# Linear attention in pairs of chunks, values held twice, and steps of attention and projection alternating

## The chip, the core and the metric

The kernel runs on one core of one Trainium2 chip. The metric is the device time of one execution in microseconds (us). The kernel before takes 1238.45 us, the median of three runs (1237.87 to 1241.02).

## What is computed

One transformer layer over x of 1 x 2048 x 512. The first part is causal linear attention on the normalized x: 16 query heads, four key/value heads (each shared by four query heads), head size 128. Queries and keys are rotated by their position (rotary map) and then go through elu + 1; a state of 128 x 128 and a vector z grow with every token:

```
q = rotary(Wq xn); k = rotary(Wk xn); v = Wv xn        # xn = layernorm(x)
qf = elu(q) + 1;   kf = elu(k) + 1
for each token s:
    state = state + outer(kf[s], v[s]);  z = z + kf[s]
    o[s] = (qf[s] . state) / (qf[s] . z + 1e-6)
x = x + Wo o
```

The second part is a mixture of 32 experts and 32 zero experts on the normalized result: softmax scores plus a bias, the top 8 per token, at most 256 tokens per expert, silu(g) * u between two matrix products, and a weighted sum added to x.

## The kernel before

*Tiling.* The 2048 tokens are cut into four blocks of 512 (`NSB`, `SB`), a block into four chunks of 128 (`NC`, `P`), and a chunk into two halves of 64 (`T`). Inside a block there is a loop over `G` = 4 groups; a group is one key/value head with its `R` = 4 query heads. Everything in the attention is f32, and a matrix product of f32 runs on TensorE as two passes, which the trace records separately.

*A block.* `norm_block` normalizes x and transposes it (xT). `values` (L266) makes the values of a chunk for all four groups (pv) and ScalarE copies them to SBUF (`va`, L274). `project` (L299) does a group: the keys pk (L305, four matmuls of 128 x 512), then `rope_feature` (L277) on them, a running sum over the tokens (zT, L309), then four times the queries of a head, pq (L317, four matmuls each), each with `rope_feature`. Then the denominators: VectorE multiplies queries by zT (qz, L325) and TensorE sums over the head with a matrix of ones (pd, L328). VectorE adds 1e-6 and takes the reciprocal (rd, L331 and L332). These are written to DRAM (`recip`, L333) and read back four times, once per chunk, spread over all 128 partitions (`rds`, L337, 256 KB each); `rds` has three buffers. Write and reloads go through SP's DMA queue, which works in order.

*`rope_feature`* takes a projection in PSUM to a feature in SBUF. VectorE multiplies by the cosine (L282), multiplies each half of 64 rows by the sine and puts it into the other half's place (L283, L284), adds (L285) and takes the minimum with 0 (L286); ScalarE takes exp of that (L287); VectorE forms max(., 0) + exp (L288).

*Attention of a chunk.* `by_token` transposes the keys of a group (L294), and ScalarE copies them (kk, L296). `attend` (L343) does a chunk: scores of each half against itself (L355, two matmuls, each on 64 columns of the array); the increments of the state, once for the first half (64 rows) and once for the whole chunk (128 rows) (L361), both in the same PSUM tile as the scores; the state's additions on VectorE (L366); the causal mask on the scores (at, L370); the output po per half, first from the state (L376, full array), then from the values (L379, 64 rows of the array); and VectorE's product with the reciprocals (oT, L381).

*After the groups.* `output` (L383) multiplies by Wo (px, L391, 16 matmuls), adds x (L393) and normalizes again; `route` (L404) transposes (prt, L408), makes the router's logits (pl, L413), softmax and top 8 (sel, L431) and each token's place in its expert's list (pp, L446 and L447); `list_further` writes the lists with indirect DMAs. These are interleaved with the fourth group of a block. After the last block come the experts (L561 on), which this change doesn't touch.

*Buffers.* pk, pq, px and pv share two PSUM buffers (`p_pj`); scores with state increments have two (`p_sc`), po one per half (`p_o`), transposes one (`p_tr`), and pd, pl and pp together one (`p_ms`).

*Order.* Each engine takes its instructions in the order that the built program gives. A framework decides it: it keeps data dependences and buffer turns, and apart from these a scheduler with its own estimates arranges the instructions of an engine, starting from the order of the source. In the source (main loop, L501 on) the projection of the next group, g + 1, comes in one piece ahead of the four chunks of group g; with g = 3 it is the next block's norm and first group.

Of the kernel before, what the change touches and what calls it, by code (L numbers as in the profile page):

```python
# [9 lines left out]
F32 = mybir.dt.float32  # L10
# [3 lines left out]
ALU = mybir.AluOpType  # L14
# [4 lines left out]
P = 128  # L19
# [33 lines left out]
def linattn_moe(  # L53
# [122 lines left out]
    with ExitStack() as ph:  # L176
        wts = ph.enter_context(tc.tile_pool(name="wts", bufs=1))
        blk = ph.enter_context(tc.tile_pool(name="blk", bufs=2))
# [3 lines left out]
        rdp = ph.enter_context(tc.tile_pool(name="rdp", bufs=NC - 1))  # L182
        rowp = ph.enter_context(tc.tile_pool(name="rowp", bufs=NC))
        vap = ph.enter_context(tc.tile_pool(name="vap", bufs=NC))
# [6 lines left out]
        p_sc = ph.enter_context(tc.tile_pool(name="p_sc", bufs=2, space=PSUM))  # L191
# [8 lines left out]
        def load_block(sb):  # L200
            xs = [load_row(sb * NC + c, "n") for c in range(NC)]
            if sb == 0:
                first_weights()
            cs = blk.tile([P, SB], F32, tag="cs", name=f"cs_{sb}")
            nc.sync.dma_start(out=cs, in_=cosT[:, ts(sb, SB)])
            sn = blk.tile([P, SB], F32, tag="sn", name=f"sn_{sb}")
            nc.sync.dma_start(out=sn, in_=sinT[:, ts(sb, SB)])
            return xs, cs, sn
# [56 lines left out]

        def values(sb, c, xT):  # L266
# [6 lines left out]
            va = vap.tile([P, G, HD], F32, tag="va", name=f"va_{sb}_{c}")  # L273
            nc.scalar.copy(va, pv)  # L274
            return va

        def rope_feature(dst, ps, sb, name):  # L277
# [3 lines left out]
            hh = HD // 2  # L281
            nc.vector.tensor_tensor(dst, ps, cs, ALU.mult)  # L282
            nc.vector.tensor_tensor(b[:hh], ps[hh:], sn[hh:], ALU.mult)  # L283
            nc.vector.tensor_tensor(b[hh:], ps[:hh], sn[:hh], ALU.mult)  # L284
            nc.vector.tensor_tensor(dst, dst, b, ALU.add)  # L285
            nc.vector.tensor_scalar(b, dst, 0.0, None, ALU.min)  # L286
            nc.scalar.activation(b, b, AF.Exp)  # L287
# [11 lines left out]
        def project(sb, g, xT):  # L299
# [11 lines left out]
            if sb < NSB - 1:  # L311
                nc.scalar.copy(zend[:, g : g + 1], zT[:, SB - 1 :])
            qT = qkp.tile([P, R, SB], F32, tag="qT", name=f"qT_{sb}_{g}")
            for r in range(R):
# [4 lines left out]
                rope_feature(qT[:, r, :], pq, sb, f"q{sb}_{g}_{r}")  # L319

# [18 lines left out]
            return kT, qT, rds  # L339
# [3 lines left out]
        def attend(sb, g, c, proj, kk, va, oT):  # L343
# [3 lines left out]
            n = f"{sb}_{g}_{c}"  # L347
            halves = range(P // T)
            half = [slice(c * P + a * T, c * P + (a + 1) * T) for a in halves]
            old = state[g]  # L350
            psk = p_sc.tile([P, R * T + 2 * HD], F32, tag="sc", name=f"psk_{n}")
            psc = psk[:, : R * T].rearrange("p (r t) -> p r t", r=R)
            pst = psk[:, R * T :].rearrange("p (a d) -> p a d", a=2)
            for a in halves:
                nc.tensor.matmul(psc[ts(a, T)], lhsT=kT[:, half[a]], rhs=qT[:, :, half[a]],  # L355
                                 start=True, stop=True)

            n_new = 2 if sb < NSB - 1 or c < NC - 1 else 1
            for a in range(n_new):
                to = slice(0, (a + 1) * T)  # L360
                nc.tensor.matmul(pst[:, a], lhsT=kk[to, c], rhs=va[to, g, :], start=True, stop=True)  # L361
            new = stp.tile([P, 2, HD], F32, tag=f"st{g}", name=f"state_{n}")
            if old is None:
                nc.vector.tensor_copy(new, pst)
            else:
                nc.vector.tensor_tensor(new[:, :n_new], pst[:, :n_new],  # L366
                                        old[:, 1:].to_broadcast([P, n_new, HD]), ALU.add)
            state[g] = new
            at = tmp.tile([P, R, T], F32, tag="at", name=f"at_{n}")
            nc.vector.tensor_tensor(at, psc, causal.unsqueeze(1).to_broadcast([P, R, T]), ALU.mult)  # L370
            pos = []
            for a in halves:
                po = p_o.tile([P, R, T], F32, tag=f"o{a}", name=f"po_{n}_{a}")
                before_half = (old[:, 1] if old is not None else None, new[:, 0])[a]
                if before_half is not None:
                    nc.tensor.matmul(po, lhsT=before_half, rhs=qT[:, :, half[a]], start=True, stop=False)  # L376
                pos.append((po, before_half is None))
            for a, (po, first) in enumerate(pos):
                nc.tensor.matmul(po, lhsT=va[ts(a, T), g, :], rhs=at[ts(a, T)], start=first, stop=True)  # L379
            for a, (po, first) in enumerate(pos):  # L380
                nc.vector.tensor_tensor(oT[:, :, half[a]], po, rds[c][:, :, ts(a, T)], ALU.mult)  # L381
# [22 lines left out]
        def route(ch, xw):  # L404
# [19 lines left out]
            sb_ = sml.tile([P, EZ], F32, tag="sbias", name=f"sbias_{ch}")  # L424
# [3 lines left out]
            rest = sml.tile([P, EZ], F32, tag="rest", name=f"rest_{ch}")  # L428
# [22 lines left out]
            if ch >= LISTED:  # L451

                free = sml.tile([P, E], F32, tag="hi", name=f"free_{ch}")
# [15 lines left out]
            hi = sml.tile([P, E], F32, tag="hi", name=f"hi_{ch}")  # L469
            nc.vector.tensor_scalar(hi, pos, float(C2), float(P * NCOL - 1), ALU.is_ge, ALU.mult)  # L470
            mi = sml.tile([P, E], F32, tag="mi", name=f"mi_{ch}")
# [378 lines left out]
```

## Time and profile before

| what | us |
|---|---|
| runs: median (lowest to highest) | 1238.45 (1237.87 to 1241.02) |
| the profiled execution itself | 1237.05 |
| its span on the engines | 1235.3 |
| first matmul / last instruction of px (end of the attention) | 9.6 / 886.7 |
| busy, whole span: TensorE / VectorE / ScalarE / GpSimd | 1050.5 / 637.9 / 130.2 / 219.7 |
| pq (L317) / px (L391), 512 records each, busy | 230.3 / 232.4 |
| po from state (L376) / from values (L379), busy | 76.8 / 54.6 |
| scores (L355) / state increments (L361), busy | 50.5 / 56.7 |
| VectorE's oT (L381), 128 instructions, busy | 50.1 |
| ScalarE's exp of a feature (L287), one | 0.630 |

The profile is that of one execution. "Busy" is the time in which an engine has an instruction in work; matmuls overlap with their neighbours, so their own durations add up to more than the time from one start to the next. A "wait" names what was last to release an idle engine; it is inferred from the semaphores' events. PEld is TensorE's loading of weights, and DMA queues are named after the engine that issues (SPq is SyncE's). In the page's row of slices the span is cut in 40 parts, and each digit is a busy share in tenths.

### The profile page before, as it was taken

How to read it: one execution, taken by the hardware profiler on the slowest of the kernel's cores; microseconds unless marked ns; L12 is line 12 of the kernel's file. 1: busy time of each engine (PE TensorE's matmuls, PEld its weight loads, DVE VectorE, ACT ScalarE, POOL GpSimd, SP SyncE). 2: the span in 40 equal slices, each digit the busy share in tenths (PEclk: the TensorE clock that was granted, in tenths of full speed). 3: DMA queues.
4: the chain of work that ended last, by engine and by line, in shares of the span. 5: the costliest groups of instructions: out<-in, count | busy, mean ns of one | idle time of the engine just before them, and what ended most of it. 6: DMA issues, size and time to landing. Idle time of an engine off the chain costs nothing. (4 is left out here: it accounts for less than half of the span.)

```text
span 1235.3 us, 13580 instructions
## 1 busy us (share of the span) xinstructions
PE 1050.5 (85%) x4410; PEld 530.9 (43%) x4410; DVE 637.9 (52%) x1553; ACT 130.2 (11%) x256; POOL 219.7 (18%) x254
## 2 busy tenths in 40 slices
PE   5999999999999899999999999999737765672772
PEld 2444444444444444444444444444312554441440
DVE  4888874358888435888843388834322111110110
ACT  1111110011121001112100111100011100110000
POOL 4000001430000343000034200023353121211211
PEclk9999999999999999999999999999967877786887
DMA  9411212100121210012321112340572484967224
GB/s 346 151 16 33 69 49 55 52 26 13 34 77 40 60 52 27 13 35 58 75 61 52 61 45 67 102 59 27 167 254 74 109 273 149 319 187 235 45 39 156
DMA packets 90840, 116.26 MB, mean 94 GB/s; under 512 B 12493, under 2 KB 47309, under 8 KB 90672
## 3 DMA queue, kind: packets, MB, share of 16 engines
q1 hardware_dynamic: 74640, 93.53, 25.5%
q0 software_dynamic: 10336, 12.51, 5.2%
q10 hardware_dynamic: 5760, 8.92, 2.0%
q8 instruction: 55, 0.90, 0.3%
q14 instruction: 49, 0.40, 0.1%
HBM read 101.35 MB, written 20.96 MB: 99 GB/s over the span
## 5 line engine op out<-in xcount | busy, mean ns | idle before, releaser
L317 PE MATMUL pq<-xT,wq 128*128 128x512 f32 x512 | 230.3, 599 | 10.1 <-DVE rb_q L284 10.1
L391 PE MATMUL px<-wo,oT 128*128 128x512 f32 x512 | 232.4, 599 | 0.0
L166 POOL DMA_INDIRECT slots<-tok,ai x120 | 117.6, 980 | 501.5 <-DVE ai L485 468.9
L317 PEld LDWEIGHTS pq<-xT,wq 128*128 128x128 f32 x512 | 94.4, 190 | 138.5 <-issue 107.3
L391 PEld LDWEIGHTS px<-wo,oT 128*128 128x128 f32 x512 | 93.9, 191 | 98.1 <-issue 97.6
L728 PE MATMUL pu<-xeT,gu 128*128 128x224 f32 (+1 forms) x352 | 69.4, 367 | 11.0 <-DVE xeT L656 9.7
L376 PE MATMUL po<-qT,state 128*128 128x256 f32 x248 | 76.8, 402 | 2.2 <-DVE oT L381 1.9
L728 PEld LDWEIGHTS pu<-xeT,gu 128*128 128x128 f32 x352 | 65.4, 230 | 15.4 <-issue 13.1
L393 DVE TENSOR_TENSOR x<-px,x 128x512 f32<-128x512 f32 x16 | 11.1, 692 | 113.6 <-PE px L391 98.8
L381 DVE TENSOR_TENSOR oT<-po,rds 128x256 f32<-128x256 f32 x128 | 50.1, 414 | 33.7 <-PE po L379 18.8
L305 PE MATMUL pk<-xT,wk 128*128 128x512 f32 x128 | 63.5, 627 | 0.7 <-ACT xT L263 0.7
L242 POOL TENSOR_TENSOR lnr<-lnv,mhalf 128x1 f32<-128x1 f32 (+1 forms) x20 | 13.3, 664 | 255.0 <-DVE lnv L240 228.8
L271 PE MATMUL pv<-wv,xT 128*128 128x512 f32 x128 | 57.7, 598 | 0.0
L361 PE MATMUL psk<-va,kk 64*128 64x128 f32 (+1 forms) x248 | 56.7, 323 | 0.0
L287 ACT ACTIVATE rb_q<-rb_q 128x512 f32<-128x512 f32 x64 | 40.3, 630 | 155.4 <-DVE rb_q L286 155.1
L376 PEld LDWEIGHTS po<-qT,state 128*128 128x128 f32 x248 | 41.2, 189 | 35.6 <-issue 21.7
L379 PE MATMUL po<-at,va 64*128 64x256 f32 x256 | 54.6, 428 | 0.0
L355 PE MATMUL psk<-qT,kT 128*64 128x256 f32 x256 | 50.5, 404 | 0.0
L361 PEld LDWEIGHTS psk<-va,kk 64*128 64x128 f32 (+1 forms) x248 | 36.8, 186 | 31.6 <-issue 23.8
L643 POOL DMA_INDIRECT acc<-y,idx x17 | 25.9, 1524 | 130.0 <-ACTq L778 40.0
L672 PE MATMUL pu_b<-gu,xeT_b 128*32 128x256 f32 x512 | 40.2, 424 | 10.0 <-issue 9.5
L325 DVE TENSOR_TENSOR qz<-qT,zT 128x512 f32<-128x512 f32 x64 | 42.4, 687 | 11.1 <-PE pd L328 10.6
(180 smaller groups left out, 1135.1 us busy)
## 6 DMA issues: line engine op xcount, KB each, us to landing
gu<-in_wgu_dram SPq DMA_DIRECT2D x32, 1024.0 KB
rds<-recip SPq DMA_DIRECT2D x64, 256.0 KB
dn<-in_wdn_dram SPq DMA_DIRECT2D x32, 512.0 KB
rows<-xw ACTq DMA_DIRECT2D x16, 272.0 KB
xn<-in_x_dram SPq DMA_DIRECT2D x16, 256.0 KB
wq<-in_wqT_dram SPq DMA_DIRECT2D x4, 1024.0 KB
wo<-in_woT_dram SPq DMA_DIRECT2D x4, 1024.0 KB
x<-in_x_dram SPq DMA_DIRECT2D x16, 256.0 KB
```

The lines of the kernel that those rows point to most:

```text
L166: nc.gpsimd.indirect_dma_start(out=slots[k][:, :], out_offset=bass.IndirectOffsetOnAxis(ap=ai[:, k : k + 1], axis=0), in_=tok[:, ch : ch + 1],
L271: nc.tensor.matmul(pvf, lhsT=xT[:, k, ts(c, P)], rhs=wv[:, k, :], start=(k == 0), stop=(k == KD - 1))
L305: nc.tensor.matmul(pk, lhsT=wk[:, k, ts(g, HD)], rhs=xT[:, k, :], start=(k == 0), stop=(k == KD - 1))
L317: nc.tensor.matmul(pq, lhsT=wq[g][:, k, ts(r, HD)], rhs=xT[:, k, :], start=(k == 0), stop=(k == KD - 1))
L325: nc.vector.tensor_tensor(qz, qT[:, :, cc], zT[:, cc].unsqueeze(1).to_broadcast([P, R, P]), ALU.mult)
L355: nc.tensor.matmul(psc[ts(a, T)], lhsT=kT[:, half[a]], rhs=qT[:, :, half[a]], start=True, stop=True)
L361: nc.tensor.matmul(pst[:, a], lhsT=kk[to, c], rhs=va[to, g, :], start=True, stop=True)
L376: nc.tensor.matmul(po, lhsT=before_half, rhs=qT[:, :, half[a]], start=True, stop=False)
L379: nc.tensor.matmul(po, lhsT=va[ts(a, T), g, :], rhs=at[ts(a, T)], start=first, stop=True)
L381: nc.vector.tensor_tensor(oT[:, :, half[a]], po, rds[c][:, :, ts(a, T)], ALU.mult)
L391: nc.tensor.matmul(px, lhsT=oTs[h // R][:, h % R, ts(c, P)], rhs=wo[h // R][:, h % R, :], start=(h == 0), stop=(h == H - 1))
L728: nc.tensor.matmul(pu[:, a, :m], lhsT=weights[e][0][:, k, a, c, :], rhs=xeT[:, k, :m], start=(k == 0), stop=(k == KD - 1))
```

## The change

Line numbers here are those of the changed file.

- Attention is done on pairs of chunks (`attending`). Scores of both chunks go to one PSUM tile (`p_sc`, now one buffer; four matmuls, L365), the increments of the state to another (`p_st`), and po of both chunks to one tile per half.
- The values are held twice (`vas`, four fixed tiles): once as before, and once with the first 64 tokens of the chunk only and zeros in the other 64 rows (cleared once by GpSimd, L271). So both increments of a chunk come from one matmul of 128 x 256 on the full array (L370). ScalarE makes two copies (L280, L281).
- In `rope_feature` ScalarE copies the two halves crossed (L288, L289), VectorE multiplies 128 rows by the sine in one instruction (L291), and relu(-x) on ScalarE (L293) takes the place of VectorE's minimum; exp then has scale -1 (L294). The sine is loaded in two halves, exchanged (L208, L209).
- `project` and `attend` become generators, `projecting` and `attending`, whose steps the loop takes in turn: the first pair's scores and states, k of the next group, the first pair's outputs, q0, q1, the second pair's scores and states, q2, q3, the second pair's outputs, and last the denominators with the reciprocal, its DMA write and the reloads (L339 to L346). Where g = 3, the outputs and the routing stand among these.
- Buffers: cosine and sine (`blk`) one instead of two, `rds` two instead of three, and one for several small tiles of the router (`sml`).

The core of the diff:

```diff
-        blk = ph.enter_context(tc.tile_pool(name="blk", bufs=2))
+        blk = ph.enter_context(tc.tile_pool(name="blk", bufs=1))
...
-        rdp = ph.enter_context(tc.tile_pool(name="rdp", bufs=NC - 1))
+        rdp = ph.enter_context(tc.tile_pool(name="rdp", bufs=2))
         rowp = ph.enter_context(tc.tile_pool(name="rowp", bufs=NC))
-        vap = ph.enter_context(tc.tile_pool(name="vap", bufs=NC))
+        vap = ph.enter_context(tc.tile_pool(name="vap", bufs=1))
...
-        p_sc = ph.enter_context(tc.tile_pool(name="p_sc", bufs=2, space=PSUM))
+        p_sc = ph.enter_context(tc.tile_pool(name="p_sc", bufs=1, space=PSUM))
+        p_st = ph.enter_context(tc.tile_pool(name="p_st", bufs=1, space=PSUM))
...
-            nc.sync.dma_start(out=sn, in_=sinT[:, ts(sb, SB)])
+            for i in range(2):
+                nc.sync.dma_start(out=sn[ts(i, HD // 2)], in_=sinT[ts(1 - i, HD // 2), ts(sb, SB)])
...
+        vas = [vap.tile([P, G, 2, HD], F32, name=f"va_{c}") for c in range(NC)]
+        for va in vas:
+            nc.gpsimd.memset(va[T:, :, 0, :], 0.0)
...
-            va = vap.tile([P, G, HD], F32, tag="va", name=f"va_{sb}_{c}")
-            nc.scalar.copy(va, pv)
-            return va
+            nc.scalar.copy(vas[c][:, :, 1, :], pv)
+            nc.scalar.copy(vas[c][:T, :, 0, :], pv[:T])
...
         def rope_feature(dst, ps, sb, name):
             _, cs, sn = blocks[sb]
             b = tmp.tile([P, SB], F32, tag="rb", name=f"rb_{name}")
             hh = HD // 2
+            nc.scalar.copy(b[:hh], ps[hh:])
+            nc.scalar.copy(b[hh:], ps[:hh])
             nc.vector.tensor_tensor(dst, ps, cs, ALU.mult)
-            nc.vector.tensor_tensor(b[:hh], ps[hh:], sn[hh:], ALU.mult)
-            nc.vector.tensor_tensor(b[hh:], ps[:hh], sn[:hh], ALU.mult)
+            nc.vector.tensor_tensor(b, b, sn, ALU.mult)
             nc.vector.tensor_tensor(dst, dst, b, ALU.add)
-            nc.vector.tensor_scalar(b, dst, 0.0, None, ALU.min)
-            nc.scalar.activation(b, b, AF.Exp)
+            nc.scalar.activation(b, dst, AF.Relu, scale=-1.0)
+            nc.scalar.activation(b, b, AF.Exp, scale=-1.0)
             nc.vector.scalar_tensor_tensor(dst, dst, 0.0, b, ALU.max, ALU.add)
...
-        def project(sb, g, xT):
+        def projecting(sb, g, xT):
...
+            yield
             qT = qkp.tile([P, R, SB], F32, tag="qT", name=f"qT_{sb}_{g}")
...
                 rope_feature(qT[:, r, :], pq, sb, f"q{sb}_{g}_{r}")
+                yield
...
-            return kT, qT, rds
+            projs[sb, g] = kT, qT, rds
+            yield
...
-        def attend(sb, g, c, proj, kk, va, oT):
+        def attending(sb, g, c0, proj, kk, oT):
             kT, qT, rds = proj
-            n = f"{sb}_{g}_{c}"
+            n = f"{sb}_{g}_{c0}"
+            chunks = range(2)
             halves = range(P // T)
-            half = [slice(c * P + a * T, c * P + (a + 1) * T) for a in halves]
-            old = state[g]
-            psk = p_sc.tile([P, R * T + 2 * HD], F32, tag="sc", name=f"psk_{n}")
-            psc = psk[:, : R * T].rearrange("p (r t) -> p r t", r=R)
-            pst = psk[:, R * T :].rearrange("p (a d) -> p a d", a=2)
-            for a in halves:
-                nc.tensor.matmul(psc[ts(a, T)], lhsT=kT[:, half[a]], rhs=qT[:, :, half[a]],
-                                 start=True, stop=True)
-            n_new = 2 if sb < NSB - 1 or c < NC - 1 else 1
-            for a in range(n_new):
-                to = slice(0, (a + 1) * T)
-                nc.tensor.matmul(pst[:, a], lhsT=kk[to, c], rhs=va[to, g, :], start=True, stop=True)
-            new = stp.tile([P, 2, HD], F32, tag=f"st{g}", name=f"state_{n}")
-            if old is None:
-                nc.vector.tensor_copy(new, pst)
-            else:
-                nc.vector.tensor_tensor(new[:, :n_new], pst[:, :n_new],
-                                        old[:, 1:].to_broadcast([P, n_new, HD]), ALU.add)
-            state[g] = new
-            at = tmp.tile([P, R, T], F32, tag="at", name=f"at_{n}")
-            nc.vector.tensor_tensor(at, psc, causal.unsqueeze(1).to_broadcast([P, R, T]), ALU.mult)
-            pos = []
-            for a in halves:
-                po = p_o.tile([P, R, T], F32, tag=f"o{a}", name=f"po_{n}_{a}")
-                before_half = (old[:, 1] if old is not None else None, new[:, 0])[a]
-                if before_half is not None:
-                    nc.tensor.matmul(po, lhsT=before_half, rhs=qT[:, :, half[a]], start=True, stop=False)
-                pos.append((po, before_half is None))
-            for a, (po, first) in enumerate(pos):
-                nc.tensor.matmul(po, lhsT=va[ts(a, T), g, :], rhs=at[ts(a, T)], start=first, stop=True)
-            for a, (po, first) in enumerate(pos):
-                nc.vector.tensor_tensor(oT[:, :, half[a]], po, rds[c][:, :, ts(a, T)], ALU.mult)
+            half = [[slice((c0 + i) * P + a * T, (c0 + i) * P + (a + 1) * T) for a in halves] for i in chunks]
+            psc = p_sc.tile([P, 2, R, T], F32, tag="sc", name=f"psc_{n}")
+            for i in chunks:
+                for a in halves:
+                    nc.tensor.matmul(psc[ts(a, T), i], lhsT=kT[:, half[i][a]], rhs=qT[:, :, half[i][a]],
+                                     start=True, stop=True)
+            pst = p_st.tile([P, 2, 2, HD], F32, tag="st", name=f"pst_{n}")
+            for i in chunks:
+                nc.tensor.matmul(pst[:, i], lhsT=kk[:, c0 + i], rhs=vas[c0 + i][:, g], start=True, stop=True)
+            seen = []
+            for i in chunks:
+                old = state[g]
+                new = stp.tile([P, 2, HD], F32, tag=f"st{g}", name=f"state_{n}_{i}")
+                if old is None:
+                    nc.vector.tensor_copy(new, pst[:, i])
+                else:
+                    nc.vector.tensor_tensor(new, pst[:, i], old[:, 1:].to_broadcast([P, 2, HD]), ALU.add)
+                state[g] = new
+                seen.append((None if old is None else old[:, 1], new[:, 0]))
+            ats = []
+            for i in chunks:
+                at = tmp.tile([P, R, T], F32, tag="at", name=f"at_{n}_{i}")
+                nc.vector.tensor_tensor(at, psc[:, i], causal.unsqueeze(1).to_broadcast([P, R, T]), ALU.mult)
+                ats.append(at)
+            yield
...
+            po = [p_o.tile([P, 2, R, T], F32, tag=f"o{a}", name=f"po_{n}_{a}") for a in halves]
+            fresh = [True, True]
+            for i in chunks:
+                for a in halves:
+                    if seen[i][a] is not None:
+                        nc.tensor.matmul(po[a][:, i], lhsT=seen[i][a], rhs=qT[:, :, half[i][a]],
+                                         start=fresh[a], stop=False)
+                        fresh[a] = False
+            for i in chunks:
+                for a in halves:
+                    nc.tensor.matmul(po[a][:, i], lhsT=vas[c0 + i][ts(a, T), g, 1, :], rhs=ats[i][ts(a, T)],
+                                     start=False, stop=(i == 1))
+            for i in chunks:
+                for a in halves:
+                    nc.vector.tensor_tensor(oT[:, :, half[i][a]], po[a][:, i], rds[c0 + i][:, :, ts(a, T)],
+                                            ALU.mult)
+            yield
...
-            sb_ = sml.tile([P, EZ], F32, tag="sbias", name=f"sbias_{ch}")
+            sb_ = sml.tile([P, EZ], F32, tag="sbias", name=f"sbias_{ch}", bufs=1)
...
-        projs = {(0, 0): project(0, 0, xTs[0])}
+        projs = {}
+        for _ in projecting(0, 0, xTs[0]):
+            pass
...
-                    vas = [values(sb, c, xTs[sb]) for c in range(NC)]
-                if g + 1 < G:
-                    projs[sb, g + 1] = project(sb, g + 1, xTs[sb])
-                elif not last:
-                    xTs[sb + 1] = norm_block(sb + 1)
-                    projs[sb + 1, 0] = project(sb + 1, 0, xTs[sb + 1])
+                    for c in range(NC):
+                        values(sb, c, xTs[sb])
                 if last and g == G - 1:
                     for i in range(2):
                         load_pair(i)
+                if g + 1 < G:
+                    ahead = projecting(sb, g + 1, xTs[sb])
+                elif not last:
+                    xTs[sb + 1] = norm_block(sb + 1)
+                    ahead = projecting(sb + 1, 0, xTs[sb + 1])
+                else:
+                    ahead = iter(())
                 oT = otp.tile([P, R, SB], F32, tag="oT", name=f"oT_{sb}_{g}")
                 oTs[sb, g] = oT
                 kk = by_token(sb, g, projs[sb, g][0])
-                for c in range(NC):
-                    attend(sb, g, c, projs[sb, g], kk, vas[c], oT)
-                    if g == G - 1:
-                        if c != 1 and waiting:
-                            route_and_list(*waiting.pop(0))
-                        if c >= 1:
-                            waiting.append((sb * NC + c - 1,
-                                            output(sb, c - 1, [oTs[sb, i] for i in range(G)])))
+                pairs = [attending(sb, g, c, projs[sb, g], kk, oT) for c in (0, 2)]
+                def routed():
+                    if waiting:
+                        route_and_list(*waiting.pop(0))
+                def put(c):
+                    waiting.append((sb * NC + c, output(sb, c, [oTs[sb, i] for i in range(G)])))
+                next(pairs[0])
+                next(ahead, None)
+                next(pairs[0])
+                if g == G - 1:
+                    routed()
+                next(ahead, None)
+                if g == G - 1:
+                    put(0)
+                next(ahead, None)
+                next(pairs[1])
+                if g == G - 1:
+                    routed()
+                    put(1)
+                next(ahead, None)
+                if g < G - 1:
+                    next(ahead, None)
+                next(pairs[1])
+                if g == G - 1:
+                    next(ahead, None)
+                next(ahead, None)
+                if g == G - 1:
+                    routed()
+                    put(2)
```

## The prediction

> **What bounds the kernel now.** I read the page's busy shares and slices first, then what TensorE waited for between 16 and 890 us, one group of the attention by engine, TensorE's timeline inside it, and the DMA queue beside the vector engine.
>
> ```profile
> PE 1050.5 (85%) x4410; PEld 530.9 (43%) x4410; DVE 637.9 (52%) x1553; ACT 130.2 (11%) x256; POOL 219.7 (18%) x254
> ...
> PE   5999999999999899999999999999737765672772
> ...
> DVE  4888874358888435888843388834322111110110
> ```
>
> For some 28 slices TensorE is full: that is the attention, from the first matmul at 9.6 us to the last px at 886.7. The remaining 348.6 us of the span (experts) aren't touched.
>
> ```profile
> PE pq L317 <- DVE rb_q L284: 10.1, 18, 1.9
> PE prt L408 <- issue: 7.8, 5, 3.3
> ```
>
> TensorE hardly waits there: some 25 us in all, 10.1 of them for a projection's PSUM buffer, which DVE frees late.
>
> ```profile
> 289.60:323.30 33.70, 33.51 (x143) 15.76 (x143) 29.34 (x55) 3.92 (x7) 0.00 (x0) 1.00 0.17 34
> ```
>
> Columns: window, length, busy PE, PEld, DVE, ACT, POOL, clock, DMA. This is one group with nothing but projection and attention (g = 1 or 2; "inner" below, eight in the run). DVE has 29.3 us in 33.7: it is the next bound, 4 us behind.
>
> ```profile
> 319.37 0.60 PE L294 MATMUL pk<-ident,kT 128*128 128x128 f32 x4
> 319.90 0.65 PE L355 MATMUL psk<-qT,kT 128*64 128x256 f32 x4
> 320.48 0.70 PE L376 MATMUL po<-qT,state 128*128 128x256 f32 x2
> 321.11 0.90 PE L361 MATMUL psk<-va,kk 64*128 64x128 f32 x4
> 321.94 0.65 PE L355 MATMUL psk<-qT,kT 128*64 128x256 f32 x4
> ```
>
> Two records are one f32 matmul. From start to start the scores take 0.58 for two matmuls, because the halves run side by side; po 0.63 for one, where an undisturbed one takes 0.43 (two passes of 0.216); the two state matmuls 0.83, where two of 128 columns are 0.44. Each passage between full, half-row, half-column and quarter-column use costs about 0.1 on leaving and 0.05 to 0.1 on entering. That is what pairing attacks.
>
> ```profile
> 49.96 0.33 SPq L333 DMA_DIRECT2D recip<-rd  x1
> 51.72 1.47 SPq L337 DMA_DIRECT2D rds<-recip  x3
> ```
> ```profile
> 807.34 9.40 SPq L337 DMA_DIRECT2D rds<-recip  x4
> ```
> ```profile
> 815.59 0.76 DVE L381 TENSOR_TENSOR oT<-po,rds 128x256 f32<-128x256 f32 x2 [5.13 <-DMA rds<-recip]
> 819.51 0.42 DVE L381 TENSOR_TENSOR oT<-po,rds 128x256 f32<-128x256 f32 x1 [0.64 <-DMA rds<-recip]
> ```
>
> The reciprocals go through DRAM: the first reload can be issued 1.8 us after the write (idle queue), and an rds issued at 807.34 let DVE go at 815.6, 8.2 us later; its neighbour, issued 0.45 later, at 819.5. Now this is mostly hidden: the reloads are asked for a whole group ahead.
>
> **What the Trainium skill says.** "TensorEngine Tiling (Array Packing)", Key Properties: changing the tiling mode drains TensorE, and different tiles run in parallel; the timeline agrees (0.309 instead of 0.216 to the next start). "ScalarE: Activation LUTs", Table sets: relu is in every set, so relu beside exp needs no table load; the listing of the changed program has none. "DMA: Bandwidth & Descriptors", Anatomy of one DMA: about 2.0 us fixed plus bytes/436e3; for 256 KB an estimate of 2.6 us. An x load of that size does land in 2.5, but rds, in 512-byte pieces, in 7.9 to 8.7: the trace is used.
>
> **The change, part by part.** I count from the order of instructions in the built program, with the trace's durations.
>
> *Pairs and doubled values (TensorE).* Passes: 0.429 for 512 columns, 0.2145 for 256, 0.109 for 128, plus the passages. Over 64 chunks, before: scores 44.8, state 47.9, po from state 67.0, po from values 48.7, sum 208.4. After: 39.6, 29.1 (one full matmul of 256 columns, no half-row one), 58.8, 40.0 (in six of 32 pairs the scheduler parts the neighbours that would run side by side), sum 167.5. Passages 424 to 236. pk and pq, cut more often, give 3.7 back. TensorE's attention work: 847.8 to 810.6, **-37.2 us**. The same count explains all but 29 us of before's 877.
>
> *Rope.* DVE loses one 64-row multiply (0.60 start to start) and the min (0.34) per feature, 4.7 us per group: about 24.6 busy. ScalarE gains two 64-row copies and a relu, 1.8 us; both unknown here: the copy bounded by 0.3 (half a 128-row copy) and 0.63, taken at its row's 0.585; relu like the exp, 0.63. ScalarE then has 12.7 us per group: hidden. But each feature's chain gets longer: multiply 0.60, multiply 0.73, add 0.69, relu and exp with handovers 1.43, last op 0.60: 4.05 us, and the listing has DVE do the next feature only after it, where before it put that feature's multiplies into the gap. In two of four features a copy stands between relu and exp: +0.5. Four features: 17.2 us against TensorE's 13.7 + 2.1 for the second pair's scores and states. Without any other wait an inner group then needs DVE 31.3 and TensorE 31.2: a balance.
>
> *The order (the decisive step).* The reciprocals of a group now come out directly before that group's first pair. On DVE the listing reads: reciprocal, the next k's five operations (5.3 us), four oT, then the first query feature. Let E be the reciprocal's end, 1.5 us after the last pd. Write: E + 1.8. First rds: E + 9.9. Second: before shows it at 11.3 to 12.1 after the first issue, with a third behind it; two alone aren't shown. Bounds 8.4 (only its later issue) and 13.8 (one after the other); I take 11.0: E + 12.8. The oT are in order, so DVE stands from E + 5.3, some 6.1 us, and behind it all four features; the third projection needs the buffer that the first feature frees, so TensorE stands too. Laid out from the last pd: oT done at 15.0, features at 32.5, the next last pd at **37.4 us per inner group, against 33.7 now**.
>
> In waits of TensorE: g = 1, 6.5 each, 26; g = 2, where the next block's transposes stand between, 8.7 three times and 7.5 in the last block, 33.6; g = 3 in the two middle blocks: the router's pp waits for sel, which stands on DVE behind the same four oT, 6.4 each, 12.8; in the last block recip of g = 2 stands in SP's queue behind 2 MB of expert weights, 5 (between 0 and 10); g = 0, where the values' 14 us cover the round trip, 0.8 each, 3.2. Sum 80.6.
>
> *Edits at nothing.* cs and sn with one buffer: their loads wait for the last query of the block, 10 us of TensorE work before they are needed, at 2.9 to 3.9 each; uncovered, 4 us per block. They and the x loads pass in front of the next recip on SP, and are done by then. Two rds buffers: the second pair's reloads have some 18 us. sn in two halves: one more issue, 0.35. Four memsets on POOL: while the first loads run. The second copy of the values: ScalarE idles there.
>
> *Sum.* Start 9.6; slow first matmuls and waits up to the second k, 8.7; work 810.6; other waits, 20.6 before (pq and prt among them), 3 left; 80.6. The last px at 912.5. With 348.6: span 1261.1; with the 1.75 around it (1237.05 against 1235.3) 1262.9; the median of the runs is 1.4 above the profiled one: **1264**.
>
> **Rivals.** *The round trip is covered* (ends on the other side): if both rds are there when the k chain is done, DVE doesn't stand, and the 37 us of passages and 10 of pq waits are gained: 9.6 + 8.7 + 810.6 + 3 + 11 + 348.6 + 3.2 gives 1195. For it: before, oT waited only 14.7 us for rds. Against: they were issued a group ahead. It decides once TensorE's new waits are under 55 us, the second rds within about E + 10. *Partly covered*: 8.4 instead of 11.0, 2.6 us in some 11 places: 1236. *Fully serial*: 13.8 and a write of 3.5, 4.5 us in 11 places: 1314. *The doubled values don't help*: if the state matmul kept its passages, 19 us of the gain go: 1283; against it, full matmuls in a row show no passage.
>
> **How the numbers follow.** Likeliest 0.71, its own range 1249 (the second rds 1.4 us earlier in 11 places) to 1284 (it at 12.1, the write 0.7 later); covered 0.15; partly 0.09, half of it within the bound; serial or no help 0.05. A measurement tells 0.3%, 3.7 us. Faster 0.19, same 0.05, slower 0.76; the range goes from the partly covered case to the likeliest's upper end, 1236 to 1284, and leaves out the covered and the serial case, 2 in 10.
>
> **What would show it.** Passes of the four attention groups near 168 us by starts; oT waiting for rds in tens of us instead of 14.7, the longest about 6; pq waiting for DVE more than 10.1; an inner group of 37, PE busy falling in those slices. I am wrong if oT doesn't wait and inner groups take 31.

## The result and the profile after

The changed kernel takes 1279.47 us (median of four runs, 1277.39 to 1281.7) against 1238.62 for the kernel before (1237.87 to 1241.02): ratio 1.0327, 95% interval 1.0304 to 1.0349. It is slower by some 41 us, where the prediction had 1264 us in a range from 1236 to 1284: right in direction and inside the range. The profiled execution has a span of 1277.2 us, 41.9 more than before. Its last px starts at 928.4 us instead of 886.7, and 348.8 us follow it instead of 348.6: the whole loss lies in the attention. Since that rest varies (335 to 352 us in the complete kernels below), the runs are also compared by their last px, each that of one profiled execution.

The page's busy shares and slices of the changed kernel:

```profile
PE 1035.2 (81%) x4290; PEld 538.0 (42%) x4290; DVE 551.0 (43%) x1393; ACT 277.2 (22%) x512; POOL 221.9 (17%) x258
...
PE   6998899999878999988799998896936855683672
...
PEclk9998999999999999998899999998957877787887
```

TensorE is busy 15 us less than before, and yet it is no longer full in the attention: the row of nines has 7s, 8s and a 6, and in four of the same slices PEclk, which was 9 throughout, falls to 8. Next, most of what TensorE waited for between 16 and 930 us (total, times, longest; pq are the query projections, psc the scores, prt the routing's transposes, pp the places in the lists, pxt the transposes of x, po the outputs). Then the vector engine's (VectorE's, DVE in the lines) wait for the reloads, first in the kernel before, then in the changed one:

```profile
PE pq L325 <- DVE qT L290: 26.1, 12, 4.6
PE psc L365 <- DVE qT L295: 12.1, 8, 1.6
PE prt L430 <- issue: 11.6, 2, 9.3
PE pp L468 <- DVE sel L453: 10.6, 3, 5.4
PE pxt L264 <- ACT xT L265: 9.7, 6, 2.6
PE po L392 <- DVE state L378: 8.4, 7, 1.7
```
```profile
DVE oT L381 <- DMA rds<-recip: 14.7, 7, 5.1
```
```profile
DVE oT L401 <- DMA rds<-recip: 78.4, 25, 6.1
```

oT waits 78.4 us for the reloaded reciprocals, where it was 14.7. All of it falls on the first pair of a group; the second pair's oT, whose reloads have to wait for the two `rds` buffers, never waits for them. One such wait, the vector engine's timeline in the third group of the first block, and SP's queue beside it (the write, and the issue of the four reloads):

```profile
129.55 0.95 DVE L341 RECIPROCAL rd<-rd 128x128 f32<-128x128 f32 x1
...
134.51 1.23 DVE L316 TENSOR_TENSOR_SCAN zT<-ones,kT 128x512 f32<-128x512 f32 x1
140.46 0.75 DVE L401 TENSOR_TENSOR oT<-po,rds 128x256 f32<-128x256 f32 x2 [4.72 <-DMA rds<-recip]
144.08 0.76 DVE L401 TENSOR_TENSOR oT<-po,rds 128x256 f32<-128x256 f32 x2 [2.87 <-DMA rds<-recip]
144.75 0.68 DVE L290 TENSOR_TENSOR qT<-pq,cs 128x512 f32<-128x512 f32 x1
```
```profile
130.53 0.33 SPq L342 DMA_DIRECT2D recip<-rd  x1
132.07 13.15 SPq L346 DMA_DIRECT2D rds<-recip  x4
```

The reciprocal ends at E = 130.5. k's operations fill 5.3 us, then the engine stands 4.7 and 2.9 us; the first query feature, already projected, starts only at 144.75. TensorE, one group earlier, stands for its buffer behind just that, and then something else follows. Its timeline, and the windows view of the same time (window, length, busy PE, PEld, DVE, ACT, POOL, granted clock, DMA share, GB/s):

```profile
101.51 1.13 PE L370 MATMUL pst<-va,kk 128*128 128x256 f32 x4
106.55 8.90 PE L325 MATMUL pq<-xT,wq 128*128 128x512 f32 x14 [3.91 <-DVE qT L290]
```
```profile
102.00:105.00 3.00, 0.64 (x3) 0.21 (x2) 0.65 (x2) 0.00 (x0) 0.00 (x0) 1.00 0.21 55
105.00:108.50 3.50, 1.96 (x3) 0.92 (x4) 2.98 (x6) 0.59 (x1) 0.00 (x0) 0.51 0.27 40
108.50:112.00 3.50, 3.50 (x6) 1.42 (x5) 2.30 (x5) 1.73 (x4) 0.00 (x0) 0.52 0.62 75
112.00:116.00 4.00, 4.00 (x11) 1.75 (x10) 2.41 (x5) 2.42 (x4) 0.00 (x0) 1.00 0.08 20
```

From 105.0 us, still inside the wait, until 111.9 the array works at half its clock: passes of 512 columns start every 0.853 us instead of 0.429. The Trainium skill describes this ("TensorE: Matmul & The Clock Gate", What's actually happening): a monitor with windows of about 3.4 us halves the clock after an idle window and frees it after a busy one. The trace agrees in the lengths: its stretches of half clock are 3.4, 6.8 and 10.2 us long. It differs in one point, the window need not be idle: in the 3.4 us before 105.0 TensorE had worked for 1.0. From 25 us on to the last px these stretches sum to 64.8 us in the changed kernel, 3.4 in the one before.

To see where the 41.7 us come from I divided the time up to the last px. Between its first matmul and the last px TensorE is busy for 849.1 us before and 835.0 after, and idle the rest. Of the busy time, 3.4 us before and 54.2 after lie in stretches of half clock; half of that is time which full clock would have saved.

| us up to the last px | before | after | difference | predicted |
|---|---|---|---|---|
| work (busy, at full clock) | 847.4 | 807.9 | -39.5 | -37.2 |
| waits (idle) | 27.9 | 83.4 | +55.5 | +63.0 |
| added by half clock (an estimate) | 1.7 | 27.1 | +25.4 | not priced |
| first matmul | 9.6 | 10.0 | +0.4 | 0 |
| last px | 886.7 | 928.4 | +41.7 | +25.8 |

(The prediction started from 847.8 us of work and 29.3 of waits before; its +63.0 is 8.7 + 3 + 80.6 - 29.3.)

### The profile page after: what moved, and what is told of

Read it like the earlier page. It is cut to its first block, busy times and chain, and to the rows that moved or that the text cites. A ratio compares the mean times of both kernels' runs of the same rounds, so it can differ in the third digit from the quotient of the medians.

```text
span 1277.2 us, 13536 instructions
## 1 busy us (share of the span) xinstructions
PE 1035.2 (81%) x4290; PEld 538.0 (42%) x4290; DVE 551.0 (43%) x1393; ACT 277.2 (22%) x512; POOL 221.9 (17%) x258
## 5 line engine op out<-in xcount | busy, mean ns | idle before, releaser
L325 PE MATMUL pq<-xT,wq 128*128 128x512 f32 x512 | 238.6, 617 | 26.1 <-DVE qT L290 26.1
L413 PE MATMUL px<-wo,oT 128*128 128x512 f32 x512 | 236.4, 612 | 0.0
L401 DVE TENSOR_TENSOR oT<-po,rds 128x256 f32<-128x256 f32 x128 | 47.5, 417 | 78.4 <-DMA rds<-recip 78.4
L293 ACT ACTIVATE rb_q<-qT 128x512 f32<-128x512 f32 x64 | 40.3, 630 | 171.1 <-DVE qT L292 171.0
L392 PE MATMUL po<-qT,state 128*128 128x256 f32 x248 | 64.3, 391 | 8.4 <-DVE state L378 8.4
L295 DVE SCALAR_TENSOR_TENSOR qT<-qT,rb_q 128x512 f32<-128x512 f32 x64 | 44.3, 692 | 60.7 <-ACT rb_q L294 60.2
L312 PE MATMUL pk<-xT,wk 128*128 128x512 f32 x128 | 68.1, 637 | 0.7 <-ACT xT L265 0.7
L288 ACT COPY rb_q<-pq 64x512 f32<-64x512 f32 x64 | 37.3, 582 | 102.9 <-PE pq L325 53.1
L392 PEld LDWEIGHTS po<-qT,state 128*128 128x128 f32 x248 | 44.7, 189 | 31.6 <-issue 13.6
L365 PE MATMUL psc<-qT,kT 128*64 128x256 f32 x256 | 45.4, 408 | 12.1 <-DVE qT L295 12.1
L290 DVE TENSOR_TENSOR qT<-pq,cs 128x512 f32<-128x512 f32 x64 | 43.9, 686 | 22.1 <-ACT rb_q L289 22.0
L695 POOL DMA_INDIRECT acc<-y,idx x17 | 25.9, 1525 | 131.8 <-ACTq L830 34.4
L292 DVE TENSOR_TENSOR qT<-qT,rb_q 128x512 f32<-128x512 f32 x64 | 44.0, 687 | 1.1
```

Source lines behind the costliest of these rows:

```text
L295: nc.vector.scalar_tensor_tensor(dst, dst, 0.0, b, ALU.max, ALU.add)
L312: nc.tensor.matmul(pk, lhsT=wk[:, k, ts(g, HD)], rhs=xT[:, k, :], start=(k == 0), stop=(k == KD - 1))
L325: nc.tensor.matmul(pq, lhsT=wq[g][:, k, ts(r, HD)], rhs=xT[:, k, :], start=(k == 0), stop=(k == KD - 1))
L365: nc.tensor.matmul(psc[ts(a, T), i], lhsT=kT[:, half[i][a]], rhs=qT[:, :, half[i][a]], start=True, stop=True)
L392: nc.tensor.matmul(po[a][:, i], lhsT=seen[i][a], rhs=qT[:, :, half[i][a]], start=fresh[a], stop=False)
L401: nc.vector.tensor_tensor(oT[:, :, half[i][a]], po[a][:, i], rds[c0 + i][:, :, ts(a, T)], ALU.mult)
```

## The experiments

Theory A: the vector engine stands for the reloads, TensorE behind it, and half clock follows. Theory B: it is the feature's longer chain through ScalarE. Ratios are to the kernel before on the same chip. What follows ran on four chips; the median of the kernel before was 1228.0, 1243.9, 1241.5 and 1239.4 us on them, so times of different chips are compared by their ratios. "By its ratio" puts a time on the chip of the first result, where the kernel before takes 1238.62 us.

**Without the wait.**

```diff
-nc.vector.tensor_tensor(oT[:, :, half[i][a]], po[a][:, i], rds[c0 + i][:, :, ts(a, T)], ALU.mult)
+nc.vector.tensor_tensor(oT[:, :, half[i][a]], po[a][:, i],
+                        ones[:, :T].unsqueeze(1).to_broadcast([P, R, T]), ALU.mult)
```

> The changed kernel, but oT multiplies po by ones; the reciprocals are still written and reloaded, only nobody reads them, so the division is left out. Theory A (the vector engine stands for the reloads, and TensorE behind it): oT's 78 us of waiting go to 0, pq's wait from 26.1 to under 8, pp's from 10.6 to under 2, the 9.3 us ahead of prt in the last block go, and with these waits the half-speed stretches before the last px, 64.8 us in the changed kernel, to under 10. Sum -26 - 10 - 9 - 15 with some 5 given back by features that are now next: 1225 us (1210 to 1240). Theory B (the longer chain of a feature through ScalarE is what TensorE waits for, whatever oT does): the waits of pq, psc and po stay, not under 1262 us.

Measured: last px 850.1, 78.3 us earlier than the changed kernel. TensorE's waits fell from 83.4 to 29.6 us, what half clock adds from 27.1 to 6.8, work by 4.2; pq's wait for the vector engine is no longer listed. The total (1166.69, ratio 0.950) doesn't count, since the routing saw other numbers and the experts had fewer matmuls (pu 224 instead of 352). A holds and I had put its size too low (by last px, 78 us against some 55), though pp's wait, 3.2 us, and the half-speed stretches, 13.7 us, stayed above the 2 and 10 expected. The 42 us that the change lost, and 37 us of gain besides, hung on this wait. Among what remains, psc 11.5 and pxt 8.9 us aren't the reloads'.

**Outputs two steps later.** The loop takes pair 0's outputs after q1, pair 1's after the denominators:

```diff
 next(pairs[0])
 next(ahead, None)
+next(ahead, None)
+next(ahead, None)
 next(pairs[0])
...
-next(ahead, None)
...
-next(ahead, None)
 next(pairs[1])
...
 next(ahead, None)
-if g < G - 1:
-    next(ahead, None)
+next(ahead, None)
+next(ahead, None)
 next(pairs[1])
-if g == G - 1:
-    next(ahead, None)
-next(ahead, None)
...
```

> The changed kernel, but each pair's outputs two steps later: the first pair's after q1 instead of after k, the second pair's after the denominators. Nothing is left out. Theory A: the first pair's reloads (13.6 us after the reciprocal) then lie behind k, q0 and q1 (13.4 us of features); the second pair's reloads are asked for later and may still cost 2 to 4 us per group. pq's wait under 12, half-speed stretches under 25 us: 1245 us (1228 to 1260). Theory B: nothing changes in the features: 1270 or more.

Measured: 1212.81 us, ratio 0.9877 (0.9852 to 0.9901), last px 873.2; oT's wait 36.6 us. By its ratio that is 1223 us: better than expected, and a complete kernel that beats both. The half-speed stretches, 37.5 us, stayed above the 25 expected. The order is a remedy, but half of the wait stays.

**Projection in one piece**, the order of before.

```diff
+for _ in ahead:
+    pass
 next(pairs[0])
-next(ahead, None)
 next(pairs[0])
...
```

> The changed kernel with the order of before: the whole projection of the next group ahead of the pairs of this one; pairs, doubled values, the new rope and the buffers stay. Theory A: the first pair's reloads are asked for a group ahead again; the second pair's wait for the two buffers, 8 to 11 us behind the first pair's oT, of which the next projections hide most. TensorE's work keeps its 33 us of gain: 1218 us (1200 to 1240). Theory B: four features in a row need 17.2 us against 13.7 of TensorE: pq waits about 3 us in each of 15 groups: 1250 or more.

Measured: 1243.65 us, ratio 1.0119 (1.0098 to 1.0140), last px 904.5. Both expectations failed in part: by its ratio the time is 1253 us, which is B's, yet the vector engine's waits are A's:

```profile
DVE oT L401 <- DMA rds<-recip: 92.7, 26, 6.4
```

Of these, 82.7 us fall on the second pair's oT: with two buffers its reloads are issued only when the first pair's oT has freed them. (That three buffers cure this was not run.) That the reloads were it, and not four features in a row, needed the next run (same order, oT times ones):

> The order of before (projection in one piece) with pairs, doubled values and new rope, oT multiplying by ones (the division is left out; the routing that follows sees other numbers, so only the time up to the last px counts). Theory A': the one-piece kernel lost because the second pair's reloads wait for the two buffers, not because of its order: oT's 92.7 us of waiting go and the last px falls from 904.5 to 850 to 862. If four features in a row were the limit, it stays above 880.

Measured (a single run): last px 853.8. So without the wait for reloads both orders end within 4 us of each other (850.1 with the steps alternating), and alternating gains little in itself.

**The rope alone** in the kernel before.

```diff
-nc.sync.dma_start(out=sn, in_=sinT[:, ts(sb, SB)])
+for i in range(2):
+    nc.sync.dma_start(out=sn[ts(i, HD // 2)], in_=sinT[ts(1 - i, HD // 2), ts(sb, SB)])
...
+nc.scalar.copy(b[:hh], ps[hh:])
+nc.scalar.copy(b[hh:], ps[:hh])
 nc.vector.tensor_tensor(dst, ps, cs, ALU.mult)
-nc.vector.tensor_tensor(b[:hh], ps[hh:], sn[hh:], ALU.mult)
-nc.vector.tensor_tensor(b[hh:], ps[:hh], sn[:hh], ALU.mult)
+nc.vector.tensor_tensor(b, b, sn, ALU.mult)
...
-nc.vector.tensor_scalar(b, dst, 0.0, None, ALU.min)
-nc.scalar.activation(b, b, AF.Exp)
+nc.scalar.activation(b, dst, AF.Relu, scale=-1.0)
+nc.scalar.activation(b, b, AF.Exp, scale=-1.0)
```

> The kernel before with the new rope alone (halves copied crossed by ScalarE, relu on ScalarE, the sine loaded with its halves exchanged). Theory A: the vector engine is relieved of 4.7 us per group, the chain gets longer by about 1.5 us per feature but attention of the group before lies beside it: 1240 us (1232 to 1250). Theory B: the rope is the main part of the loss: 1260 or more.

Measured: 1222.05 us, ratio 0.9948 (0.9931 to 0.9965), last px 880.0: a small gain (by its ratio 1232 us, the lower edge of A's range). B falls as the main cause. The reverse, the changed kernel with the rope of before (the same diff backwards):

> The changed kernel with the rope of before (two 64-row multiplies and the minimum on the vector engine, exp alone on ScalarE). Theory A: the stand for the reloads stays (oT 65 to 85 us); the vector engine has 4.7 us more per group, of which some falls into its standing: ratio to before 1.03 to 1.05, last px 925 to 945. If the rope's longer chain is what costs in the alternating order: under 1.015.

Measured: 1271.85 us, ratio 1.0235 (1.0203 to 1.0267), last px 918.4, oT's wait 72.7. This lies between the two expectations. Most of the loss remains, as A says; but 10 us of it were the rope's, more than expected: in the alternating order the longer chain does cost, where in the order of before it didn't.

**The reload itself.** A chunk's four rows of reciprocals are laid side by side, so that each partition reads one piece:

```diff
-recip = [[dram.tile([R, SL, P], F32, ...
+recip = [[dram.tile([SL, R, P], F32, ...
...
-nc.sync.dma_start(out=recip[sb][g].rearrange("r m t -> (r m) t"), in_=rd)
+nc.sync.dma_start(out=recip[sb][g].rearrange("m r t -> r m t"), in_=rd)
...
-nc.sync.dma_start(out=t, in_=recip[sb][g][:, c, :].unsqueeze(0).to_broadcast([P, R, P]))
+nc.sync.dma_start(out=t.rearrange("p r t -> p (r t)"),
+                  in_=recip[sb][g][c].rearrange("r t -> (r t)").unsqueeze(0).to_broadcast([P, R * P]))
```

> The changed kernel, but the reciprocals of a chunk's four heads lie side by side in DRAM, so that a reload reads one piece of 2 KB per partition instead of four of 512 bytes. Nothing is left out, the order is the same. An x load of the same 256 KB in 2 KB rows landed in 2.6 to 4.4 us where a reload took 7.7 to 11.6. Theory A: if the reload becomes like the x load, the first one is there about 6 us after the reciprocal and the second at 7 to 8, against 5.3 us of k's operations: oT's wait falls from 78 us to 15 to 30, the last px from 928.4 to 855 to 870, ratio to before 0.965 to 0.98. If the size of the pieces is not what the reload's time comes from: unchanged, 1.03.

Measured: 1201.81 us, ratio 0.9674 (0.9643 to 0.9706), last px 854.6. The first four reloads in this trace land 3.1 to 3.4 us after their issue, instead of 7.7 to 10.7. The same group as above, on the vector engine and on SP's queue:

```profile
122.47 0.95 DVE L341 RECIPROCAL rd<-rd 128x128 f32<-128x128 f32 x1
...
129.25 1.42 DVE L402 TENSOR_TENSOR oT<-po,rds 128x256 f32<-128x256 f32 x4 [0.60 <-DMA rds<-recip]
130.59 0.68 DVE L290 TENSOR_TENSOR qT<-pq,cs 128x512 f32<-128x512 f32 x1
```
```profile
123.45 0.52 SPq L342 DMA_DIRECT2D recip<-rd  x1
125.88 5.14 SPq L346 DMA_DIRECT2D rds<-recip  x4
```

The 7.6 us of standing have become 0.6, though the write takes longer (2.4 us to the first reload's issue, before 1.5); over the run oT waits 3.9 us for reloads, less than the 15 to 30 expected. This is the changed kernel with its order, its buffers and its rope: only the layout of the reciprocals in DRAM differs, and with it the size and number of the pieces. The Trainium skill ("DMA: Bandwidth & Descriptors", Specifications) gives 512 bytes as the least transfer for full rate; the measurement decides otherwise here. For 256 KB, 128 pieces of 2 KB took 3.0 to 3.7 us over the whole run and 512 pieces of 512 bytes 7.6 to 12.2. While the first two slow reloads were under way (132.07 to 140.40 us) the core's DMA moved 50 GB/s with its engines busy 19% of the time; for the quick ones (125.9 to 129.2 us) it was 156 GB/s and 57%. Would the kernel before have gained as much?

> The kernel before with the packed reciprocals alone (reload in 2 KB pieces). There oT waits only 14.7 us for reloads, and hardly any of it reaches TensorE: last px 881 to 886, ratio 0.993 to 1.0. If the gain of the packed changed kernel (0.967) were the reload's own and not that of pairs, doubled values and order, it would be under 0.98 here too.

Measured: 1232.65 us, ratio 0.9939 (0.9914 to 0.9963), last px 881.8. No: there the reloads were hidden. So the rest of the gain belongs to the rest of the change, which the reloads had covered up: above all TensorE's work at full clock, 803.8 us in the packed changed kernel against 847.4 in the kernel before. Pairs and doubled values were not run alone, so what each of them is worth isn't shown.

**The array kept busy.**

```diff
 for i in chunks:
-    nc.tensor.matmul(pst[:, i], ...)
+    for _ in range(6 if g in (1, 2) and c0 == 2 and i == 1 else 1):
+        nc.tensor.matmul(pst[:, i], ...)
```

> The changed kernel, but in groups 1 and 2 of each block the last of the second pair's state matmuls is done six times over (each overwrites the one before with the same values), 5 x 0.43 = 2.15 us of useless work just ahead of the projection that waits 1.1 to 4.6 us for its buffer: 17 us in all. If the half-speed stretches come from TensorE standing idle, those after these waits (105 to 112, 146 to 149, 552 to 556 and 590 to 597 us) vanish and give back some 8 us, while the added work lies in the waits: last px 921 (918 to 927), ratio to before 1.027. If TensorE's speed has another cause, the time is unchanged or grows with what of the 17 us does not fit: last px 928 to 935.

Measured: 1275.35 us, ratio 1.0258 (1.0234 to 1.0281), last px 929.7. Three of the four stretches are gone; the one at 145 stayed. The window from 105 to 112 us now has its full clock:

```profile
105.00:112.00 7.00, 5.04 (x11) 2.12 (x12) 5.41 (x11) 2.32 (x4) 0.00 (x0) 1.00 0.45 59
```

In the sum the work rose by 18.5 us, waits fell by 8.2, what half clock adds by 9.0: the last px is 1.3 us later, not the 921 expected but in the range of the other theory. The clock itself decides between them: where the idling was filled, it stayed full, so idling is what halves it. (At 145 us, in the 3.4 us ahead of the stretch that stayed, TensorE still worked for 0.8 us only.) That filling the waits pays is not shown, since my 17 us were too many for them (po's listed wait rose from 8.4 to 12.1).

**What is next late.** In the packed kernel psc waits 11.2 us for the last feature. Two edits against it: the minimum back on the vector engine in place of ScalarE's relu, and k ahead of the first scores in the source (with q0 ahead of the first outputs).

> The packed changed kernel with the minimum on the vector engine again in place of ScalarE's relu (crossed copies stay). Per feature ScalarE loses 0.63 and two handovers, the vector engine gains 0.34: the chain falls from 4.05 to some 3.65 us, and with it the 1.5 us per group that the first scores wait for the last feature. Theory A: last px 846 to 853 (854.6 with relu). If the vector engine's busy time is what bounds a group instead: 856 to 862.

Measured: 1183.38 us, ratio 0.9543 (0.9503 to 0.9582), last px 833.0. The first line is of the packed kernel, the second of this one:

```profile
PE psc L366 <- DVE qT L295: 11.2, 9, 1.6
```
```profile
PE psc L366 <- DVE qT L295: 2.0, 6, 0.8
```

That is 21.6 us, where at most 9 had been expected. TensorE's waits fell by 8.5 us, almost all of it this one, what half clock adds by 6.4, and work by 6.6: the scheduler left more half-row neighbours side by side (po from values 34.1 us by starts instead of 40.4), which I hadn't foreseen. So not all of this gain is the relu's.

> The packed changed kernel with the next group's k ahead of the first pair's scores in the source, and q0 ahead of its outputs: the wait of the scores for the last feature (12.5 us in nine places) is covered by k. Last px 844 to 850, ratio to before 0.955 to 0.964. If the wait only moves (the vector engine's chain of 31 us per group is the bound): 853 to 858.

Measured: 1193.95 us, ratio 0.9629 (0.9606 to 0.9652), last px 841.3, a little better than expected. And all three together:

> Packed reciprocals, the minimum on the vector engine and the scores after k in the source, all three. If both edits remove the same wait (that of the first scores for the last feature, 12.5 us before either, 1.8 after the minimum alone), nothing is left for the order to gain: last px 830 to 835, ratio to before 0.951 to 0.958. If the order also takes slack out of the vector engine's chain: under 828.

Measured: 1185.63 us, ratio 0.9566 (0.9532 to 0.9600), last px 835.4: both edits remove the same wait, and their gains don't add. The packed kernel with the minimum on the vector engine has the lowest ratio, though its interval overlaps with the last one's; by the last px it is 54 us ahead of the kernel before.

## Why the prediction was right, and where its sizes were off

*Pairs and doubled values.* Right: TensorE's work fell by 39.5 us, 37.2 predicted. By starts, with waits and half clock taken out, scores, states and po took some 210 us before and 170 after (208.4 and 167.5 predicted).

*Rope.* ScalarE's 12.7 us per inner group are 12.67, the copies 0.582 each and relu 0.630, as taken. From one feature to the next the chain takes 4.5, 4.8 and 4.5 us (starts at 144.75, 149.26, 154.09 and 158.61), 4.6 on average; the prediction's four make 4.3. That term was somewhat too small, and with the reloads out of the way the relu in it costs more than its price (854.6 against 833.0, of which 6.6 us is less work for TensorE).

*The order.* Right, and the decisive step. First oT at E + 9.96 (predicted 9.9), third at E + 13.6 (12.8, bound 13.8), standing 7.6 us (6.1), the eight inner groups 37.9 to 40.0 us from last pd to last pd (37.4). The 33.7 us that the prediction set beside this run from pk to pk; from last pd to last pd the kernel before takes 32.4 to 32.6 us in five of them and 34.4 to 34.5 in three, so a group lost some 5 us and not 4. By the same mark TensorE stood idle for 22.8 us in the four groups with g = 1 and 27.2 with g = 2, before 2.5 and 4.4, so 20 and 23 more (26 and 33.6 predicted); pp's two waits in the middle blocks were 10.5 (12.8). The waits were over-priced, by 7.5 us in all.

*The last block* was under-priced: from 845 us on TensorE waited 13.5 us instead of 4.5 in the same part before, 9.0 more, where I had 5, and by another path. GpSimd's and TensorE's timelines there:

```profile
860.47 0.97 POOL L166 DMA_INDIRECT slots<-tok,ai  x1 [129.20 <-DVE ai L507]
...
870.38 0.59 POOL L244 TENSOR_TENSOR lnr<-lnv,mhalf 128x1 f32<-128x1 f32 x1
```
```profile
871.61 1.11 PE L430 MATMUL prt<-ident,xw 128*128 128x128 f32 x4 [9.35 <-issue]
```

oT stood for its reloads until 858.5, and with it the routing's last operation (ai); so GpSimd's eight indirect DMAs started at 860.5, and the next chunk's normalization (lnr) stood behind them, and behind that the transposes prt. The wait had gone from VectorE through GpSimd's queue to TensorE, and the step had named only SP's. What it had named is there too, but small: the write at 806 us landed after 3.8 us, the others after 1.5.

*The step that was missing.* A wait of TensorE was priced at its own length. It also halves the clock around its end: an estimated 25.4 us more than before. With the other sizes, 25.4 - 2.3 (work) - 7.5 (waits) + 0.4 (start) is 16.0, against 15.9 from the 912.5 predicted to 928.4. So the direction and the path were understood, but part of the closeness is luck: the over-priced waits made up for some of the half clock that had no price.

*The rivals.* "The round trip is covered" was rightly the one that would decide: with quick reloads it happens, and its last px (9.6 + 8.7 + 810.6 + 3 + 11 = 842.9) compares with 854.6. "The doubled values don't help" is refuted by the state matmuls (47.9 us before, 30.0 after, by starts). The 2.6 us that the prediction worked out and then dropped for the trace's figure rest on a formula which the Trainium skill fits to DMAs that GpSimd issues ("DMA: Bandwidth & Descriptors", Anatomy of one DMA); the reloads are SyncE's, and took 3.0 to 3.7 us in 2 KB pieces.

*Open.* Why 512-byte pieces are so slow isn't settled: the DMA engines were busy only a fifth of that time. That the loss of the order alone is zero rests on runs whose oT multiplied by ones.

## What to carry to other kernels

Before moving a producer next to its consumer, follow the value by its whole route: here eight microseconds of reload, hidden while asked for a group ahead, turned a gain of some 40 us of work into a loss of 41. Look at the shape of the transfer before the order around it: four pieces laid side by side gave back 74 us at the last px, more than any order tried. Price a wait of TensorE above its own length, since what follows may run at half clock: here 25 us on top of 55.

## What was unexpected of the hardware

- A 256 KB reload took 7.6 to 12.2 us in 512-byte pieces and 3.0 to 3.7 in 2 KB pieces, for the same amount of data.
- Every stretch of half clock, in all fourteen traces, begins and ends on a fixed grid of 3.413 us. They go by how much TensorE works within one step of this grid: in the changed kernel each of the twelve stretches follows a step with at most 1.7 us of work (over all traces 1.8), and every step at full clock with less than 1.4 us of work brought one; in between both happen. So equal waits can differ: the 2.57 us from 549.1 left 0.84 us of work in their step and halved the clock at 552.2; the 2.58 us from 779.5 fell across two steps, with 2.07 and 2.17 us of work, and didn't.
- Useless matmuls in the waits kept the clock up in three of four places, at a net cost of 1.3 us.
